# A planned clock for every engine, table lookups in VectorE's waits, and norms turned by VectorE and transfers

## The chip, the cores and the metric

One core of a Trainium2 chip. The metric is the device time of one execution in microseconds (us), the median of several runs. PE is TensorE, PEld its weight loads, DVE VectorE, ACT ScalarE, POOL GpSimd, SP the engine that issues most DMAs.

## The reference

Four layers, each wrapped the same way, over x of 2 x 512 tokens with 256 features, all in float32:

```python
x = x + layernorm(attention(layernorm(x), wq, bq, ...))   # 16 heads of 128, rope, causal softmax
x = x + layernorm(gelu_ffn(layernorm(x), packed 4-bit gate, up, down))   # 2048 hidden
x = x + layernorm(linear_attention(layernorm(x), W_qkv, W_out))
x = x + layernorm(silu_ffn(layernorm(x), lut[gate_idx], lut[up_idx], lut[down_idx]))  # 688 hidden
```

The linear attention takes `q = elu(q)+1`, `k = elu(k)+1` and running sums of `k` and of `k*v` along the tokens. It returns `q*sum(k*v)/(q*sum(k)+1e-9)`, projected by W_out. The last layer's three weight matrices are drawn from a table of 16 floats by 4-bit indices, so that each weight is a lookup.

## The kernel before

The tokens are cut into four units of 256 (`NUNIT`, `TU`); two units make one batch. An activation that TensorE multiplies has features on partitions and tokens along the free dimension: `xT1`, `xT2`, `xT3` for the gelu layer, the linear attention and the silu layer, each a tile of 128 partitions x 2 chunks x 256 tokens.

**The attention** is a loop of 34 slots (`slot`, L794), one head of one batch in each. A slot issues the score matmuls of head i, VectorE's masked minimum (L645), the exponentials (L663), the projections of q and k of head i+1 with rope (L584 to L620), the scaling by the inverse sums (L851), the output projection of head i-2, the values' sum of head i-1 (`attended`, L690), and last the turn of p: VectorE transposes in 32 x 32 blocks (L677), and four DMAs (L683) carry the blocks into `pT`. GpSimd adds the two halves of rope (L619, `qT` and `kT`), which the next slot's scores need. In the last slots, half blocks of the gelu layer's first unit fill TensorE.

**The later layers** run through generators. `ffn_hidden(u)` (L741) issues gate and up products of a unit in pairs of chunks, each pair with one gelu on ScalarE (L763) and one product on VectorE (L764). `ffn_out(u)` (L769) issues 64 matmul records of the down product and then begins a chain. `run` (L1038) steps through them, and after each step calls `poll` and issues one or two steps of the table lookups (`look_up`, L295). `silu_hidden` and `silu_out` do the same for the last layer.

**A chain** is a generator of small dependent work that is not on TensorE's main path. `after_ffn(u)` (L786) runs the norm (`norms`, L182) and then `linear_attention(u)` (L902), whose end is the norm of stage 3. `yield t` says that the next piece is due t us later. `poll` (L97) continues whatever is due by `now`, a clock that only TensorE's own matmuls move on (L118 to L124). The waits are fixed numbers such as 1.7, 2.4, 4.0, and 1.3 times as long while lookups remain (`slow`, L178). The order of all instructions on each engine is the order in which the program issues them.

**The norm between two layers** (L182 to L207) takes statistics of y for two halves of 128 tokens, adds the scaled y to x, takes statistics of the sum, normalises into `ln` on ScalarE (L197), and turns it: four TensorE transposes into PSUM (L200 to L203) and one ScalarE copy into `xT` (L204). Each unit has three such norms, twelve in all: stage 1 after the attention, 2 after the gelu layer, 3 after the linear attention. The small GpSimd steps of a norm are L167, L169 (a power) and L171.

**The lookups.** `wg` (2 pieces) is made during the attention by 16 compare-and-add steps each (L236 on VectorE, L240 on GpSimd), one or two per slot. `wu` (4 pieces of 320 columns) and `wd` (3 pieces of 512) are made by selection (`select_in`, L244): 19 VectorE instructions each, masks (L262, L279), eight pairs (L265) and seven picks (L275). They are issued after the attention, one or two after each TensorE step, whatever VectorE has to do. All must be done when the silu layer begins.

PSUM has four tags (`mm`, `s`, `t`, `o`) of two banks each. An output bank `o` of the last layer comes free when VectorE has added its scaled content to x (L176).

Of the kernel before, what the change touches and what calls it, by code (L numbers as in the profile page):

```python
# [34 lines left out]
NUNIT = B * NT // HT  # L35
INTER = 688
# [5 lines left out]
EARLY = 2  # L42
REST = INTER - (NO - 1) * P


@with_exitstack
def sandwich_kernel(
# [34 lines left out]

    def bank(tag):
        return psum.tile([P, 512], F32, tag=tag, name=f"ps_{tag}")
# [33 lines left out]
    def matmul(out, lhsT, rhs, start, stop, **more):  # L118
        nc.tensor.matmul(out, lhsT=lhsT, rhs=rhs, start=start, stop=stop, **more)  # L119
        now[0] += (math.prod(rhs.shape[1:]) / 0.6 + 5) / 1e3  # L120

    def transpose(out, in_):
        nc.tensor.transpose(out, in_, ident)  # L123
        now[0] += 0.11  # L124
# [3 lines left out]
    for t in range(NT):  # L128
        (nc.scalar if t % 2 else nc.sync).dma_start(
            out=x0[0][:, t, :], in_=x[0][t * P : (t + 1) * P, :]  # L130
        )
    cols_sb = const.tile([P, 3 * NH + 2 * NK], F32, name="cols_sb")
    nc.scalar.dma_start(out=cols_sb, in_=cols)
# [11 lines left out]
    nc.gpsimd.memset(mhalf, -0.5)  # L145

    nc.scalar.activation(small.tile([P, 1], F32, tag="ve", name="early"), mhalf[:, :1], AF.Identity)
# [10 lines left out]


    def stats(y, eps):  # L160
# [3 lines left out]
        nc.vector.bn_stats(st, y)  # L164
        nc.vector.bn_aggr(mv, st)
        ve = small.tile([P, 1], F32, tag="ve", name="ve")
        nc.gpsimd.tensor_scalar(ve, mv[:, 1:2], eps, None, ALU.add)  # L167
        rstd = small.tile([P, 1], F32, tag="rstd", name="rstd")
        nc.gpsimd.tensor_tensor(rstd, ve, mhalf[:, :1], ALU.pow)  # L169
        shift = small.tile([P, 1], F32, tag="shift", name="shift")  # L170
        nc.gpsimd.tensor_scalar(shift, mv[:, 0:1], rstd, -1.0, ALU.mult, ALU.mult)  # L171
        return rstd, shift

    def add_scaled(x, y, rstd):

        nc.vector.scalar_tensor_tensor(x, y, rstd, x, ALU.mult, ALU.add)  # L176

    def slow(t):  # L178

        return 1.3 * t if terms else t  # L180

    def norms(u, y, stage, to, eps=EPS, strided=False):  # L182
# [5 lines left out]
        yield 4.0 if terms and late else 1.7  # L188
# [4 lines left out]
        yield 5.0 if terms and late else 2.4  # L193
        n = acts.tile([P, HT, D], F32, tag="ln", name=f"ln{stage}_{u}")
        for j in range(HT):
            rstd, shift = second[j]
            nc.scalar.activation(n[:, j, :], x[j], AF.Identity, bias=shift, scale=rstd)  # L197
        yield 2.0 if terms and late else 1.3
        pt = bank("t")
        for kc in range(NK):  # L200
            for j in range(HT):
                part = n[:, j, kc::NK] if strided else n[:, j, kc * P : (kc + 1) * P]
                transpose(pt[:, kc * TU + j * P : kc * TU + (j + 1) * P], part)  # L203
        nc.scalar.copy(to.rearrange("p k t -> p (k t)"), pt)  # L204
        for j in range(HT):
            nc.scalar.activation(x[j], x[j], AF.Identity, bias=first[j][1])
        yield 0.6  # L207
# [11 lines left out]
    def look_up_in(scratch, pieces):  # L219
# [5 lines left out]
        def fetch(j):  # L225
            if j < len(pieces):
                nc.sync.dma_start(out=ix[j], in_=pieces[j][0])
# [3 lines left out]
        def term(j, i):  # L231
# [4 lines left out]
            nc.vector.tensor_scalar(  # L236
                e, ix[j], float(i), lut_sb[:, i : i + 1], ALU.is_equal, ALU.mult
            )
            if i:
                nc.gpsimd.tensor_add(to, to, e)  # L240
# [3 lines left out]
    def select_in(scratch, pieces):  # L244
# [4 lines left out]
        ix = [scratch[:, j % 2, : n[j]].bitcast(I32) for j in range(len(pieces))]  # L249
        words = lut_sb.bitcast(I32)  # L250

        def fetch(j):
            if j < len(pieces):
                nc.sync.dma_start(out=ix[j], in_=pieces[j][0])

        def piece(j):
            to = pieces[j][1].bitcast(I32)
            m0, m1, m2, *s = (scratch[:, 2 + i, : n[j]].bitcast(I32) for i in range(6))
            m3 = ix[j]

            def mask(m, bit):
                return lambda: nc.vector.tensor_scalar(m, ix[j], 1 << bit, None, ALU.bitwise_and)  # L262

            def pair(t, i):
                return lambda: nc.vector.tensor_scalar(  # L265
# [8 lines left out]
            def pick(t, m, other):  # L274
                return lambda: nc.vector.copy_predicated(t, m, other)  # L275

            def first():
                fetch(j + 1)
                nc.vector.tensor_scalar(  # L279
# [3 lines left out]
            return [  # L283
# [6 lines left out]

        fetch(0)
        for j in range(len(pieces)):
            terms.extend(piece(j))
# [8 lines left out]
    with ExitStack() as at:  # L302
# [9 lines left out]
        def load(name, gg):  # L312
# [6 lines left out]
            nc.sync.dma_start(out=wts[name, gg], in_=src[gg % NG])  # L319
# [3 lines left out]
        nc.sync.dma_start(out=cos_sb, in_=cos)  # L323
# [814 lines left out]
```

## Time and profile before

| | us |
|---|---|
| median of 3 runs (lowest, highest) | 647.89 (647.65, 648.43) |
| the profiled execution | 647.38 |
| its span, first to last instruction | 645.6 |
| its time outside the span | 1.8 |
| VectorE, ScalarE and GpSimd busy in it | 477.6, 302.2, 280.9 |

[...] A float32 matmul thus shows as two records (64 of `ps_o` for one unit's down product), while a transpose is one record. A record's duration is longer than the step from its start to the next record's start, because matmuls overlap: 128x256 records have a mean of 379 ns and follow each other at 216 ns. So what TensorE's work costs is read from the steps between starts, and a lost piece of time is a step that is longer than its kind's usual one.

### The profile page before, as it was taken

What the parts mean: (1) busy time and instruction counts of PE and PEld (TensorE: products, weight loads), DVE (VectorE), ACT (ScalarE), POOL (GpSimd) and SP (SyncE); (2) the same over time, 40 slices, a digit from 0 to 9 for tenths busy, and PEclk for the clock granted to TensorE, in tenths of its full rate; (3) what the DMA queues carried; (4) which work ended last, traced back from release to release, by engine and by line L of the source; (5) the groups of instructions that cost most, each with busy time, mean ns of one, the idle gap of its engine ahead of it and who ended that gap; (6) DMA issues with size and microseconds to landing.
All of it is one profiled execution on the core that took longest, in us unless ns stands there. A gap on an engine that the chain in (4) does not pass through costs nothing.

```text
span 645.6 us, 8157 instructions
## 1 busy us (share of the span) xinstructions
PE 628.7 (97%) x2542; PEld 467.9 (72%) x2542; DVE 477.6 (74%) x1107; ACT 302.2 (47%) x662; POOL 280.9 (44%) x342
## 2 busy tenths in 40 slices
PE   8899999999999999999999999999999999989896
PEld 6566666666666666666666788888888878868785
DVE  7869889877987988888787521874984995954743
ACT  3645666666555557566655721145026025225120
POOL 3344657454453565755675200441142152253531
PEclk9999999999999999999999999999999999989999
DMA  7456474555547455464534322000000000000000
GB/s 245 118 139 186 112 198 121 134 156 138 164 110 197 121 138 152 120 152 137 137 104 89 88 53 86 11 1 11 10 8 18 0 16 2 2 0 1 24 17 24
DMA packets 35754, 57.16 MB, mean 89 GB/s; under 512 B 4096, under 2 KB 23168, under 8 KB 35712
## 3 DMA queue, kind: packets, MB, share of 16 engines
q1 hardware_dynamic: 34992, 55.94, 32.5%
q10 hardware_dynamic: 720, 0.72, 0.5%
q8 instruction: 20, 0.33, 0.2%
q14 instruction: 22, 0.18, 0.1%
HBM read 28.33 MB, written 1.05 MB: 46 GB/s over the span
## 4 chain that ended last, share of the span: by engine, by line
PE 79%; DVE 12%; POOL 3%; ACT 3%; issue 2%; DMA 1%; ACTq 0%; POOLq 0%; DVEq 0%
PE ps_mm L119 32%; PE ps_s L119 17%; PE ps_o L119 15%; PE ps_t L119 12%; DVE scratch L265 1%; DVE den L957 1%; PE ps_t L123 1%; DMA pT<-turned 1%; DVE scratch L275 1%; POOL rstd L169 1%; PE ps_o L339 1%; DVE wd L275 1%; DVE rr L611 1%; DVE ra L608 1%; DVE st L164 1%
## 5 line engine op out<-in xcount | busy, mean ns | idle before, releaser
L240 POOL TENSOR_TENSOR wg<-wg,scratch 128x752 f32<-128x752 f32 x30 | 53.4, 1779 | 97.0 <-DVE scratch L236 97.0
L119 PE MATMUL ps_mm<-xT,wg 128*128 128x256 f32 (+1 forms) x352 | 85.1, 379 | 0.3 <-ACT q L926 0.3
L663 ACT ACTIVATE p<-p,mn 128x512 f32<-128x512 f32 (+3 forms) x128 | 70.6, 553 | 30.8 <-DVE mn L645 30.8
L119 PE MATMUL ps_s<-xT,wu 128*128 128x256 f32 x336 | 81.0, 379 | 0.0
L119 PE MATMUL ps_o<-wd,hT 128*128 128x256 f32 x352 | 77.9, 379 | 1.6 <-DVE x L176 1.6
L645 DVE CUSTOM_DVE_ANT_0 p<-ps_s,mask 128x512 f32<-128x512 f32 (+2 forms) x96 | 46.2, 510 | 40.1 <-PE ps_s L119 39.9
L119 PE MATMUL ps_t<-pT,v 128*128 128x512 f32 (+3 forms) x256 | 74.3, 433 | 1.5 <-DMA pT<-turned 1.5
L119 PEld LDWEIGHTS ps_o<-wd,hT 128*128 128x128 f32 x352 | 66.7, 190 | 11.0 <-DVE x L176 2.0
L119 PEld LDWEIGHTS ps_mm<-xT,wg 128*128 128x128 f32 (+1 forms) x352 | 66.3, 189 | 9.7 <-ACT q L926 0.7
L119 PEld LDWEIGHTS ps_s<-xT,wu 128*128 128x128 f32 x336 | 63.6, 190 | 8.5
L119 PEld LDWEIGHTS ps_t<-pT,v 128*128 128x128 f32 x256 | 48.6, 190 | 28.9 <-issue 15.3
L851 ACT ACTIVATE p<-p,rs 128x512 f32<-128x512 f32 (+3 forms) x128 | 61.4, 551 | 11.7 <-DVE rs L582 9.7
L119 PEld LDWEIGHTS ps_o<-wo,oT 128*128 128x128 f32 x256 | 48.6, 190 | 19.0 <-issue 13.6
L619 POOL TENSOR_TENSOR qT<-ra,rr 128x512 f32<-128x512 f32 x32 | 40.8, 1274 | 49.3 <-DVE rr L614 47.2
L119 PE MATMUL ps_s<-kT,qT 128*128 128x512 f32 (+2 forms) x192 | 60.8, 452 | 0.2 <-DVE kT L619 0.2
L119 PE MATMUL ps_o<-wo,oT 128*128 128x256 f32 x256 | 60.5, 379 | 0.0
L119 PE MATMUL ps_mm<-xT,wk 128*128 128x512 f32 x124 | 58.4, 593 | 0.6 <-ACT v L639 0.6
L119 PE MATMUL ps_mm<-xT,wq 128*128 128x512 f32 (+1 forms) x128 | 58.4, 580 | 0.2 <-ACT xT L420 0.2
L677 DVE STREAM_TRANSPOSE turned<-p 128x512 f32<-128x512 f32 (+3 forms) x128 | 54.1, 480 | 2.1 <-DMA pT<-turned 1.0
L119 PEld LDWEIGHTS ps_s<-kT,qT 128*128 128x128 f32 x192 | 35.9, 190 | 26.6 <-issue 16.0
L119 PE MATMUL ps_mm<-wv,xTv 128*128 128x256 f32 x232 | 54.9, 379 | 0.0
L764 DVE TENSOR_TENSOR hT<-ge,ps_s 128x512 f32<-128x512 f32 x32 | 21.9, 683 | 44.1 <-PE ps_s L119 33.9
(136 smaller groups left out, 1002.5 us busy)
## 6 DMA issues: line engine op xcount, KB each, us to landing
pT<-turned SPq DMA_DIRECT2D x126, 208.0 KB, 3.8
wo<-in_wo SPq DMA_DIRECT2D x17, 256.0 KB, 4.0
wq<-in_wq SPq DMA_DIRECT2D x16, 256.0 KB, 4.1
wk<-in_wk SPq DMA_DIRECT2D x16, 256.0 KB, 5.0
wv<-in_wv SPq DMA_DIRECT2D x16, 256.0 KB, 4.1
pk_g<-in_gate_p SPq DMA_DIRECT2D x4, 256.0 KB, 5.0
sc_g<-in_gate_s SPq DMA_DIRECT2D x4, 256.0 KB
pk_u<-in_up_p SPq DMA_DIRECT2D x4, 256.0 KB, 4.5
```

Of the source, the lines that this page charges most:

```text
L119: nc.tensor.matmul(out, lhsT=lhsT, rhs=rhs, start=start, stop=stop, **more)
L123: nc.tensor.transpose(out, in_, ident)
L164: nc.vector.bn_stats(st, y)
L169: nc.gpsimd.tensor_tensor(rstd, ve, mhalf[:, :1], ALU.pow)
L240: nc.gpsimd.tensor_add(to, to, e)
L275: return lambda: nc.vector.copy_predicated(t, m, other)
L619: (nc.gpsimd if i > 1 or kind == "q" else nc.vector).tensor_add(to, a, r)
L645: nc.vector.tensor_tensor_reduce(out=p[:, p_at[it] : p_at[it] + n], in0=ps, in1=mask[:, S - n :], scale=-scale, scalar=3e38, op0=ALU.add, ...
L663: nc.scalar.activation(pi, pi, AF.Exp, bias=mn[:, it : it + 1], scale=-1.0, accum_out=sums[i][:, it : it + 1],)
L677: nc.vector.transpose(turned[:, :, 3 * it : 3 * it + n, :].rearrange("p j t b -> p t j b"), p[:, p_at[it] : p_at[it] + n * P].rearrange("p ...
L764: nc.vector.tensor_mul(hT1[u][:, c2 : c2 + 2, :].rearrange("p c t -> p (c t)"), ge, pu)
L851: nc.scalar.mul(pi, pi, rs[i][:, it : it + 1])
```

## The change

An account of each engine's time takes the place of the single clock. `vector`, `scalar`, `pool` and `sync` wrap the four engines: every instruction issued through them is given a start (when its inputs are there and its engine is free[...]) and a cost from a table by kind and length; DMAs count 0.45 or 0.8 us to issue and 3.4 to land. Matmuls enter the same account. Chains no longer wait fixed times: `yield until(...)` waits until the account says that the named tiles are written.

The selection steps of `wu` and `wd` become `fills` of VectorE. Ahead of any VectorE instruction that would start late by the account, `fill` issues as many steps as fit before it, less 0.1 us. `wu` moves into the attention, from slot 17 on, in five pieces of 256 columns, with the first batch's `xT0` and `xTv` as scratch; `wd` stays after it. `flush` issues what is left: `wu` after the attention's slots, `wd` ahead of the silu layer. `wg` is made as before.

A norm is turned another way where `late` is filled (after the attention's slots) and it is not the last unit's stage 3. By the code these are nine of the twelve: two of stage 1, four of stage 2, three of stage 3 (the change's own words say ten). VectorE transposes 32 x 32 blocks into `tr`, and four DMAs on SP carry them into `xT`, as for p. The features then lie in another order on the partitions, so the host reorders the weights' rows, and the matmuls read `xT` through a strided view (`chunk`). The scales of the packed weights need two DMAs in place of one for gate and up. A norm that TensorE still turns has two smaller ScalarE copies.

Smaller edits: `values(1, 0)` is issued ahead of the first turn of p, the loads of the third q and k weights after the first `attended`; the reciprocal and product at the end of the linear attention go in four parts of 128 columns in place of two of 256; `silu_hidden`, `ffn_out` and `silu_out` yield more often, so that chains can come in between; up to four steps of the next `silu_hidden` in place of two are issued ahead of `silu_out`.

```diff
+    def start(self, who, outs, ins):
+        at = 0.0
+        for ap in (*outs, *ins):
+            name, lo, hi = self.part(ap)
+            at = max(at, self.floor.get(name, 0.0))
+            for a, b, end, write, by in self.seen.get(name, ()):
+                if by != who and a < hi and lo < b and (write or any(ap is o for o in outs)):
+                    at = max(at, end + 0.12)
+        return at
...
+class Engine:
+    def __init__(self, who, engine, times):
+        self.who, self.engine, self.times = who, engine, times
...
+    def cost(self, name, n, more, psum):
+        if self.who == "DVE":
+            if n <= 4:
+                return 0.15
+            return {
+                "tensor_scalar": 0.17 + n / (960 if psum else 1950),
...
+    def fill(self, until):
+        self.filling = True
+        while self.fills:
+            us, reads, write = self.fills[0]
+            if self.busy + us > until or (reads is not None and self.times.written(reads) > self.busy):
+                break
+            self.fills.popleft()
+            write()
+        self.filling = False
...
+            if name == "dma_start":
+                self.busy = max(self.busy, start) + (0.8 if len(outs) + len(ins) == 2 else 0.45)
+                self.times.add("DMA", self.busy + 3.4, outs, ins)
+                return write(*args, **more)
+            if self.fills and not self.filling:
+                self.fill(start - 0.1)
+            start = max(start, self.busy)
+            if self.other and not psum and name in Engine.HELD:
+                for a, b in self.other.spans:
+                    if a <= start < b:
+                        start = b
...
     def matmul(out, lhsT, rhs, start, stop, **more):
         nc.tensor.matmul(out, lhsT=lhsT, rhs=rhs, start=start, stop=stop, **more)
+        now[0] = max(now[0], times.start("PE", [out], [lhsT, rhs]))
         now[0] += (math.prod(rhs.shape[1:]) / 0.6 + 5) / 1e3
+        times.add("PE", now[0], [out], [lhsT, rhs])
     def transpose(out, in_):
         nc.tensor.transpose(out, in_, ident)
-        now[0] += 0.11
+        now[0] = max(now[0], times.start("PE", [out], [in_])) + 0.11
+        times.add("PE", now[0], [out], [in_])
+    def until(*aps):
+        return max(0.0, times.written(*aps) - now[0])
...
+    def chunk(t, kc):
+        return t[:, :, kc].rearrange("p a j t -> p j a t")
...
         x = [xs[u][:, j, :] for j in range(HT)]
         first = [stats(t, eps) for t in y]
-        yield 4.0 if terms and late else 1.7
+        yield until(*(t for f in first for t in f))
         second = []
         for j in range(HT):
             add_scaled(x[j], y[j], first[j][0])
             second.append(stats(x[j], EPS))
-        yield 5.0 if terms and late else 2.4
+        yield until(*(t for f in second for t in f))
         n = acts.tile([P, HT, D], F32, tag="ln", name=f"ln{stage}_{u}")
+        by_blocks = late and (u, stage) != (NUNIT - 1, 3)
         for j in range(HT):
             rstd, shift = second[j]
-            nc.scalar.activation(n[:, j, :], x[j], AF.Identity, bias=shift, scale=rstd)
-        yield 2.0 if terms and late else 1.3
-        pt = bank("t")
-        for kc in range(NK):
+            to_n, from_x = n[:, j, :], x[j]
+            if not by_blocks:
+                to_n = to_n.rearrange("p (k f c) -> p k f c", k=NK, c=4)
+                from_x = from_x.rearrange(
+                    "p (c f k) -> p k f c" if strided else "p (k c f) -> p k f c", k=NK, c=4
+                )
+            elif strided:
+                to_n = to_n.rearrange("p (k m) -> p k m", k=NK)
+                from_x = from_x.rearrange("p (m k) -> p k m", k=NK)
+            scalar.activation(to_n, from_x, AF.Identity, bias=shift, scale=rstd)
+        yield until(n)
+        if by_blocks:
+            tr = acts.tile([P, 4, NK, HT, 32], F32, tag="ln", name=f"tr{stage}_{u}")
             for j in range(HT):
-                part = n[:, j, kc::NK] if strided else n[:, j, kc * P : (kc + 1) * P]
-                transpose(pt[:, kc * TU + j * P : kc * TU + (j + 1) * P], part)
-        nc.scalar.copy(to.rearrange("p k t -> p (k t)"), pt)
+                vector.transpose(
+                    tr[:, :, :, j, :], n[:, j, :].rearrange("p (k c f) -> p c k f", k=NK, c=4)
+                )
+            for a in range(4):
+                sync.dma_start(
+                    out=to[:, a].rearrange("p k j t -> p (k j t)"),
+                    in_=tr[32 * a : 32 * a + 32].rearrange("f c k j t -> f c (k j t)"),
+                )
+        else:
+            pt = bank("t")
+            for kc in range(NK):
+                for j in range(HT):
+                    transpose(
+                        pt[:, kc * TU + j * P : kc * TU + (j + 1) * P],
+                        n[:, j, kc * P : (kc + 1) * P],
+                    )
+                scalar.copy(
+                    to[:, :, kc].rearrange("p a j t -> p j a t"),
+                    pt[:, kc * TU : (kc + 1) * TU].rearrange("p (j a t) -> p j a t", j=HT, a=4),
+                )
         for j in range(HT):
-            nc.scalar.activation(x[j], x[j], AF.Identity, bias=first[j][1])
-        yield 0.6
+            scalar.activation(x[j], x[j], AF.Identity, bias=first[j][1])
+        yield until(to)
...
+            picks = (4, 8, 9, 13, 16, 17, 18)
+            one, two = 0.19 + n[j] / 960, 0.17 + n[j] / 1950
+            return [
+                (one if i in picks else two, None if i else ix[j], step) for i, step in enumerate(steps)
+            ]
         fetch(0)
         for j in range(len(pieces)):
-            terms.extend(piece(j))
+            vector.fills.extend(piece(j))
...
+            if i == NH + 1:
+                flat = [
+                    [t.rearrange("p k c -> p (k c)") for t in (up_i, wu)],
+                    [t[0].rearrange("p k s -> p (k s)") for t in (xT0, xTv)],
+                ]
+                parts = [[t[:, at : at + TU] for at in range(0, t.shape[-1], TU)] for t in flat[1]]
+                select_in(
+                    parts[0] + parts[1],
+                    [tuple(t[:, at : at + TU] for t in flat[0]) for at in range(0, NK * FULL * P, TU)],
+                )
             now_in, done = i < NS, not (jobs or behind)
...
+            if i == 0:
+                values(1, 0)
+            elif i == 1:
+                load("q", 2)
+                load("k", 2)
...
+    vector.flush()
...
+        yield until(den)
         for ch in range(NK):
-            nc.vector.reciprocal(den[:, ch, :], den[:, ch, :])
-            nc.gpsimd.tensor_mul(lT[:, ch, :], v[:, ch, :], den[:, ch, :])
-            yield slow(1.9)
-        yield slow(2.0)
+            for t in range(HT):
+                part = ch, slice(t * P, (t + 1) * P)
+                vector.reciprocal(den[:, *part], den[:, *part])
+                pool.tensor_mul(lT[:, *part], v[:, *part], den[:, *part])
+                yield 0.3
+        yield until(lT)
...
```

## The prediction

> **What bounds the kernel now.** I read the page's engine shares and slices first, then the waits of TensorE, then the timeline of TensorE where those waits are, last the windows by stage.
>
> ```profile
> PE 628.7 (97%) x2542; PEld 467.9 (72%) x2542; DVE 477.6 (74%) x1107; ACT 302.2 (47%) x662; POOL 280.9 (44%) x342
> ...
> PEclk9999999999999999999999999999999999989999
> ```
>
> TensorE is busy 97% of the span, so only two things are to be had: work that leaves TensorE, and its few lost pieces. Adding up every matmul record at its kind's usual step (109 ns for 128 columns, 216 for 256, 429 for 512) gives 618.1 us. The remaining 27.5 of 645.6 are 1.4 before the first record, about 6 after the last one's start, and 20.0 of steps that are longer than usual. Of these 20.0, 8.6 lie before 35 us (warm-up, the first head); 11.4 lie behind 245 us. The waits show whom TensorE waited for:
>
> ```profile
> engine line waited for: us in total, times, longest us
> PE ps_t L123 <- ACT ln L197: 4.9, 4, 1.9
> PE ps_o L119 <- DVE x L176: 1.6, 1, 1.6
> ```
>
> The first row is the norms' transposes, placed in TensorE's order before ScalarE had their input. The timeline of TensorE shows the worst place, behind the last gelu unit:
>
> ```profile
> start us, us, engine line op out<-in xcount [idle before <-releaser]
> 569.04 1.03 PE L119 MATMUL ps_s<-xT,wu 128*128 128x256 f32 x4
> 572.00 0.33 PE L123 MATMUL ps_t<-ident,ln 128*128 128x128 f32 x1 [1.93 <-ACT ln L197]
> 573.32 0.90 PE L123 MATMUL ps_t<-ident,ln 128*128 128x128 f32 x3 [0.99 <-ACT ln L197]
> 574.01 3.16 PE L119 MATMUL ps_o<-wout_sb,lT 128*128 128x256 f32 x8
> 577.01 1.89 PE L119 MATMUL ps_mm<-xT,wqkv_sb 128*128 128x256 f32 x8
> ```
>
> Four records from 569.04 take 0.86, four transposes 0.45: TensorE loses 574.01 - 569.90 - 0.45 = 3.7. The eight records at 574.01 then take 3.00 in place of 1.73, as the clock granted in 572 to 577 is 0.66: another 1.3. Together 5.0.
>
> ```profile
> 606.51 0.59 PE L119 MATMUL ps_o<-wout_sb,lT 128*128 128x256 f32 x2
> 607.42 1.56 PE L119 MATMUL ps_o<-wout_sb,lT 128*128 128x256 f32 x6 [0.31 <-POOL lT L958]
> 610.63 2.86 PE L119 MATMUL ps_o<-wd,hT 128*128 128x256 f32 x12 [1.64 <-DVE x L176]
> ...
> 621.96 0.60 PE L123 MATMUL ps_t<-ident,ln 128*128 128x128 f32 x4
> ```
>
> Here are 0.5 for `lT` and 1.9 for an output bank that VectorE frees late. The rest of the 11.4: 1.4 at 529.6 and 1.6 at 248 to 273 (transposes that wait for `ln`), 0.6 at 583, and small ones.
>
> **Part 1: nine norms leave TensorE.**
>
> ```profile
> 430.91 1.06 PE L123 MATMUL ps_t<-ident,ln 128*128 128x128 f32 x8
> 431.81 1.89 PE L119 MATMUL ps_s<-xT,wu 128*128 128x256 f32 x8
> ```
>
> Eight transposes move the next matmul 0.90 us, so one costs 0.11. Nine norms by four: 36 x 0.11 = **-4.0**, on the bound engine, so all of it counts. Nine ScalarE copies (583 ns) go too, beside other work. Added are 18 VectorE transposes of 256 columns (403 ns in the rows of L677 by shape, so 7.3 us), which fit where VectorE idles (part 3), and 36 DMAs on SP. What those take is in the view of the tile `turned`, the same pattern with 208 KB:
>
> ```profile
> L683 SPq DMA_DIRECT2D pT<-turned x126: 543/642/1229, 24.6 to 380.5; - x126
> ...
> DMA to landing us min/median/max: 3.3/3.8/6.1
> ```
>
> Four issues of 0.64 one behind the other and 3.8 to land: the last lands some 5.7 behind the transposes, 6.5 behind `ln`, where transposes and copy took 0.45 + 0.58 plus TensorE's turn. [...] By the rows, only a norm on which TensorE waits pays for that; the others have 50 us of a unit's matmuls to hide in. One could pay: stage 2 of the last unit. I follow the rows, and test that one in part 2.
>
> Behind the new waits of SP stand index pieces of `wd` and output rows, which nobody needs soon. The strided view of `xT` costs nothing: `attended` reads `pT` with runs of 32 too, and its 512-column records step at 429 ns like the rest. The extra scale DMAs (8 at about 0.7 of SP) are issued ahead of p's turn, and SP then waits for VectorE anyhow; unhidden they would cost 0.7 in eight slots, below the 1.6 and more by which p lands early there.
>
> **Part 2: chains by account.** The last unit's chain sets whether TensorE can stay full behind the gelu layer. Before: `ffn_out(3)` ends at 563.2, first `wqkv` 577.0, the last at 587.2, `lT` and `wout` 606.5 to 609.0, transposes 622.0: 59 us. TensorE's own work in it is three silu units (11 products of 0.86 and 5.2 out: 14.7 each, 44), `wqkv` 5.2, two `wout` 3.5, transposes 1.3: 54 us. So it must idle, and the losses above are that.
>
> After, from the same rows. Stage 2: statistics, then six GpSimd steps per half (0.22, 0.57, 0.26 with gaps, 1.13 a set) to `ln` at 6.1; transposes, DMAs 6.5: about 13, against 13.8 now; the longer turn only eats what the waits in TensorE's order gave away. Linear attention: three projections with ScalarE between, 8.7; copy, table load 1.28, two exponentials 0.62: 11.8; GpSimd's sum 13.5; scans, products, scans 18.1; four reciprocals (3.5 in all) with GpSimd's quarter products 22.3; `wout` 24.5. Before it took 32, since 57 `wd` steps held VectorE up and fixed waits were too long. Stage 3 stays on TensorE: 8. Sum 46, and TensorE then has about 52 to do. It becomes the bound in this stage, with 6 to spare.
>
> So I take off: the 5.0 at 570 to 577 (**-5.0**), the 1.4 at 529.6, a norm that leaves TensorE (**-1.4**), 1.0 of the 1.6 at 248 to 273 (those norms stay on TensorE, but ask for the account's end of `ln` instead of 1.3 us) (**-1.0**), and 2.0 of the 3.1 at 583 to 611 (**-2.0**). The bank at 610.63 I leave half: silu's second output half needs the bank of the first whenever a `wout` takes the other, and an account sees that wait but does not remove it.
>
> What the exact waits may add: eight places (`wqkv` and `wout` of four units) where TensorE is now sent to data at the predicted end. Bounds: 0 (landing counted at 3.2 + 3.4 = 6.6 against 5.7 above) and 0.5 each, 4.0. I take **+0.8**, nearest the 0.5 of `lT` at 606.5 for one or two.
>
> **Part 3: lookups into VectorE's waits.** VectorE's room by stage:
>
> ```profile
> core 0: us, PE busy (x) PEld busy (x) DVE busy (x) ACT busy (x) POOL busy (x), PEclk, DMA share, GB/s
> 247.00:365.00 118.00, 117.11 (x426) 76.82 (x425) 93.54 (x226) 72.78 (x171) 71.45 (x61) 1.00 0.48 120
> 365.00:405.00 40.00, 40.00 (x180) 33.30 (x179) 11.10 (x26) 12.27 (x24) 0.81 (x3) 1.00 0.25 72
> 405.00:563.00 158.00, 156.82 (x740) 137.60 (x739) 123.06 (x255) 51.09 (x86) 50.20 (x96) 1.00 0.03 8
> ```
>
> `wu`'s rows add up to 35.0 busy (320 columns), so 95 shorter steps are about 37 for 24 + 29 us of room: enough, with some left to the flush. A flush of up to 10 us delays the last hidden product, which `ffn_out(0)` needs some 10 us later. Behind 405 VectorE loses 35 of its 123 and gains 7. On the path all this costs nothing while a step ends before VectorE's input comes. If the account is late, the next: GpSimd's `kT` (L619, 1.27) ends only 0.37 or 0.77 ahead of the first score matmul of alternate slots. Bounds: 0 and 0.5 in each of 15 slots, 7.5. A bound below nothing is excluded, as TensorE has no wait there. I take **+0.5**: the account's costs lie near the steps of the rows (pick of 320: 0.52 by formula, 513 ns).
>
> **Start.** `values(1,0)` ahead of p's first turn takes off ScalarE's 0.6 wait at 27, but TensorE waits at 31 for the same `pT`, whose ScalarE DMAs then issue 0.5 later. Bounds -1.7 (that wait gone) and +0.5; I take 0. The finer yields and quarter products are in part 2.
>
> **Sum.** -4.0 - 5.0 - 1.4 - 1.0 - 2.0 + 0.8 + 0.5 = -12.1. Span 645.6 - 12.1 = 633.5; outside it 1.8: 635.3 for a profiled execution. The median lay 0.5 above the profiled one: **635.8**.
>
> **Rivals.** *Everything works* (0.12): no new waits, the bank's 1.1 and the start's 1.7 gained too: 635.8 - 1.3 - 1.1 - 1.7 = 631.7, down to 631. *The last chain still binds* (0.14): if transfers and GpSimd's small steps make it 56 or more in place of 46, TensorE idles 4 or more of the 7 taken off there, and 2 elsewhere: 640 to 644. For it speaks that GpSimd's rows of a set are unchanged; against it that 10 us are then to be found. *The account does not meet the chip* (0.03): new waits of the size of the old, only part of the transposes' 4.0 gained, within 1 of 647.9. *Fills hold up rope* (0.07), the slower side: [...] (the longest L265 record is 1489 ns, the median 444), so that two such steps in a slot put `kT` 2 us late: less the slack, 1.4 by 15 slots = 21, against 12.1 gained: about 656. It decides from 0.8 us of TensorE wait per slot on.
>
> **Chances.** The forecast case (633 to 639) has 0.64. Faster by over 0.2%: 0.12 + 0.64 + 0.14 = 0.90; within 0.2%, about what a measurement of this kernel can tell from no change: 0.03; slower: 0.07. The range 631 to 641 takes the forecast, the better case and part of the third.
>
> **What would show it.** L123 with `ln` falls from 48 records to 12; no idle over 1 us in TensorE behind 405 except for one bank; `wqkv` of the last unit about 13 behind the end of its down product, `wout` about 24 behind that; L265 records between 237 and 405, none of `wu` behind 415. Fills are wrong if TensorE's waits list `kT` or `pT` behind 240; the chain is wrong if TensorE idles for `xT` or `lT` behind 560.

## The result and the profile after

| us | before | after |
|---|---|---|
| median (lowest, highest), 4 runs each on one chip | 647.77 (647.32, 648.43) | 637.94 (637.14, 639.89) |
| ratio to before, 95% interval | | 0.9852 [0.9828, 0.9876] |
| the profiled execution, and its span | 647.38, 645.6 | 638.02, 636.2 |

The change gains 9.8 us in the medians, where 12.1 were forecast. The span is 9.4 shorter. The page of the changed kernel:

```profile
PE 622.6 (98%) x2506; PEld 463.1 (73%) x2506; DVE 487.8 (77%) x1152; ACT 299.6 (47%) x656; POOL 275.1 (43%) x350
...
PEclk9999999999999999999999999999999999999999
```

TensorE has 36 records less (2542 to 2506): nine norms of four transposes. No slice of the span shows a granted clock below 0.9 any more (PEclk, in tenths; a digit is a fortieth of the span). In the changed kernel the wrappers give all instructions of an engine one line: L181 are VectorE, ScalarE and GpSimd, L163 the DMAs, L272 the matmuls, L278 the transposes. Its waits of TensorE, to be set beside the two rows of `ln` and `x` in the prediction:

```profile
engine line waited for: us in total, times, longest us
PE ps_t L278 <- ACT xT L181: 2.1, 3, 0.8
...
PE ps_o L272 <- DVE x L181: 1.5, 2, 1.1
...
PE ps_mm L272 <- ACT si L181: 0.7, 1, 0.7
...
PE ps_t L278 <- ACT ln L181: 0.2, 1, 0.2
PE ps_s L272 <- DVE kT L181: 0.2, 1, 0.2
```

The wait for `ln` fell from 4.9 to 0.2. A new one for `xT` stands in first place, and the bank (`ps_o`, freed by `x`) is about where it was. The timeline of TensorE shows both, with the last unit's chain:

```profile
257.85 0.38 PE L278 MATMUL ps_t<-ident,ln 128*128 128x128 f32 x2
259.06 0.44 PE L278 MATMUL ps_t<-ident,ln 128*128 128x128 f32 x2 [0.82 <-ACT xT L181]
...
573.11 3.62 PE L272 MATMUL ps_o<-wd,hT 128*128 128x256 f32 x16
576.57 1.89 PE L272 MATMUL ps_mm<-xT,wqkv_sb 128*128 128x256 f32 x8
...
590.41 1.13 PE L272 MATMUL ps_mm<-xT,wg 128*128 128x256 f32 x4 [0.73 <-ACT si L181]
...
603.91 1.99 PE L272 MATMUL ps_o<-wout_sb,lT 128*128 128x256 f32 x8 [1.15 <-DVE x L181]
...
611.44 2.86 PE L272 MATMUL ps_o<-wd,hT 128*128 128x256 f32 x12 [0.36 <-DVE x L181]
614.14 0.27 PE L278 MATMUL ps_t<-ident,ln 128*128 128x128 f32 x1
614.58 0.33 PE L278 MATMUL ps_t<-ident,ln 128*128 128x128 f32 x1 [0.17 <-ACT ln L181]
615.37 0.44 PE L278 MATMUL ps_t<-ident,ln 128*128 128x128 f32 x2 [0.46 <-ACT xT L181]
```

`wqkv` at 576.57 now follows the product before it without idling: the 5.0 at 570 to 577 is gone. The first pair of rows is new. In the norms that TensorE still turns, the changed loop copies chunk 0 into `xT` between the second and the third transpose, and the third waits for that copy: 0.99 beyond the usual step here, the same at 293, 0.68 at 615.

To see where the time went I took each step from one matmul record's start to the next, and counted what exceeds its kind's usual step, by stage. (The usual steps are taken 1 ns low, 215 for most 256-column records of 216. This puts some 2 us into each sum, 0.7 of it into the stage from 400 to 550, alike in all runs; differences stand.)

| lost pieces of TensorE, us | to 40 | 40 to 400 | 400 to 550 | from 550 | sum |
|---|---|---|---|---|---|
| before | 6.27 | 2.94 | 2.39 | 8.38 | 19.98 |
| after | 5.92 | 3.38 | 0.77 | 4.74 | 14.81 |

The 9.4 of the span are thus 3.9 of transposes gone (36 by 0.108), 5.2 of lost pieces and 0.3 behind the last record's start. That lookups left this stage shows in the window from 405 to 560, where VectorE was busy 123.06 of 158 before (405 to 563):

```profile
core 0: us, PE busy (x) PEld busy (x) DVE busy (x) ACT busy (x) POOL busy (x), PEclk, DMA share, GB/s
405.00:560.00 155.00, 155.00 (x720) 136.24 (x719) 100.51 (x203) 47.38 (x79) 47.70 (x104) 1.00 0.06 14
```

TensorE has no gap there at all.

### The profile page after: what moved, and what is told of

The parts are those of the page before. It is cut to its first block, busy times and chain, and to the rows that moved or that the text cites. A ratio compares the mean times of both kernels' runs of the same rounds, so it can differ in the third digit from the quotient of the medians.

```text
span 636.2 us, 8205 instructions
## 1 busy us (share of the span) xinstructions
PE 622.6 (98%) x2506; PEld 463.1 (73%) x2506; DVE 487.8 (77%) x1152; ACT 299.6 (47%) x656; POOL 275.1 (43%) x350
## 4 chain that ended last, share of the span: by engine, by line
PE 91%; DVE 4%; ACT 1%; DMA 1%; issue 1%; POOL 1%; ACTq 0%; POOLq 0%; DVEq 0%
PE ps_mm L272 37%; PE ps_s L272 20%; PE ps_o L272 20%; PE ps_t L272 13%; DMA pT<-turned 1%; PE ps_o L535 1%; DVE rr L181 1%; DVE den L181 1%; PE ps_t L278 0%; DVE x L181 0%; DVE st L181 0%; ACT L181 0%; DVE ra L181 0%; DVE ks L181 0%; POOL rstd L181 0%
## 5 line engine op out<-in xcount | busy, mean ns | idle before, releaser
L181 POOL TENSOR_TENSOR wg<-wg,scratch 128x752 f32<-128x752 f32 x30 | 53.5, 1784 | 98.7 <-DVE scratch L181 98.7
L181 DVE SCALAR_TENSOR_TENSOR rr<-ps_mm,cols_sb,sin_sb 64x512 f32<-64x512 f32 (+1 forms) x126 | 93.4, 741 | 2.6 <-ACT ra L181 0.2
L272 PE MATMUL ps_mm<-xT,wg 128*128 128x256 f32 (+1 forms) x352 | 85.4, 380 | 0.8 <-ACT si L181 0.7
L181 ACT ACTIVATE p<-p,mn 128x512 f32<-128x512 f32 (+3 forms) x128 | 70.6, 553 | 30.4 <-DVE mn L181 30.4
L272 PE MATMUL ps_s<-xT,wu 128*128 128x256 f32 x336 | 81.0, 379 | 0.0
L272 PE MATMUL ps_o<-wd,hT 128*128 128x256 f32 x352 | 78.2, 379 | 0.4 <-DVE x L181 0.4
L272 PE MATMUL ps_t<-pT,v 128*128 128x512 f32 (+3 forms) x256 | 74.3, 433 | 1.9 <-DMA pT<-turned 1.9
L272 PEld LDWEIGHTS ps_o<-wd,hT 128*128 128x128 f32 x352 | 66.8, 190 | 9.8 <-DVE x L181 0.8
L272 PEld LDWEIGHTS ps_mm<-xT,wg 128*128 128x128 f32 (+1 forms) x352 | 66.1, 189 | 10.7 <-ACT si L181 1.1
L181 DVE CUSTOM_DVE_ANT_0 p<-ps_s,mask 128x512 f32<-128x512 f32 (+2 forms) x96 | 46.0, 510 | 32.0 <-PE ps_s L272 31.6
L272 PEld LDWEIGHTS ps_s<-xT,wu 128*128 128x128 f32 x336 | 63.8, 190 | 8.7
L272 PEld LDWEIGHTS ps_t<-pT,v 128*128 128x128 f32 x256 | 48.6, 190 | 29.3 <-issue 15.3
L181 ACT ACTIVATE p<-p,rs 128x512 f32<-128x512 f32 (+3 forms) x128 | 61.4, 550 | 11.2 <-DVE rs L181 9.2
L272 PEld LDWEIGHTS ps_o<-wo,oT 128*128 128x128 f32 x256 | 48.6, 190 | 19.0 <-issue 13.6
L181 POOL TENSOR_TENSOR qT<-ra,rr 128x512 f32<-128x512 f32 x32 | 40.8, 1276 | 48.4 <-DVE rr L181 46.3
L272 PE MATMUL ps_s<-kT,qT 128*128 128x512 f32 (+2 forms) x192 | 60.8, 452 | 0.2 <-DVE kT L181 0.2
L272 PE MATMUL ps_o<-wo,oT 128*128 128x256 f32 x256 | 60.5, 379 | 0.0
L272 PE MATMUL ps_mm<-xT,wq 128*128 128x512 f32 (+1 forms) x128 | 58.4, 580 | 0.2 <-ACT xT L181 0.2
L272 PE MATMUL ps_mm<-xT,wk 128*128 128x512 f32 x124 | 58.3, 592 | 0.0
L181 DVE STREAM_TRANSPOSE turned<-p 128x512 f32<-128x512 f32 (+3 forms) x128 | 54.1, 481 | 2.1 <-DMA pT<-turned 1.0
L272 PEld LDWEIGHTS ps_s<-kT,qT 128*128 128x128 f32 x192 | 36.0, 190 | 26.8 <-issue 16.0
L272 PE MATMUL ps_mm<-wv,xTv 128*128 128x256 f32 x232 | 54.9, 379 | 0.0
```

The costliest lines, as they stand in the source:

```text
L181: return write(*args, **more)
```

## The experiments

My theory: the gain is TensorE's own work taken off, plus chains that end in time. The rivals are named at each group. All edits are to the changed kernel; ratios are to the kernel before, run on the same chip with the experiments of the same batch (its medians there 646.57 for e1 to e4, 647.03 for e5 to e8, 647.53 for e9 to e12). Between batches I compare ratios, 0.001 being 0.65 us.

| | median | ratio [95%] | lost: to 40 | 40-400 | 400-550 | from 550 |
|---|---|---|---|---|---|---|
| after | 637.94 | 0.9852 [0.9828, 0.9876] | 5.92 | 3.38 | 0.77 | 4.74 |
| e1 copies behind | 636.55 | 0.9842 [0.9820, 0.9864] | 7.81 | 1.32 | 0.78 | 4.50 |
| e2 wout in another bank | 637.35 | 0.9859 [0.9836, 0.9881] | 5.49 | 3.41 | 0.77 | 3.48 |
| e3 both | 634.17 | 0.9805 [0.9786, 0.9824] | 5.88 | 1.32 | 0.77 | 3.22 |
| e4 e1, all norms on TensorE | 653.27 | 1.0098 [1.0075, 1.0122] | 6.31 | 1.32 | 12.63 | 4.18 |
| e5 e4, slower account | 637.54 | 0.9857 [0.9840, 0.9874] | 5.99 | 1.35 | 0.97 | 2.11 |
| e6 e3, slower account | 641.25 | 0.9921 [0.9900, 0.9942] | 5.66 | 1.33 | 0.64 | 10.43 |
| e7 e3, last norm by transfers | 639.89 | 0.9897 [0.9877, 0.9917] | 5.57 | 1.33 | 0.78 | 8.94 |
| e8 fixed waits | 645.77 | 0.9980 [0.9967, 0.9992] | 7.74 | 6.91 | 2.94 | 5.72 |
| e9 e6, last unit on TensorE | 639.43 | 0.9875 [0.9860, 0.9890] | 7.57 | 1.34 | 0.64 | 6.42 |
| e10 e5, wout in another bank | 637.23 | 0.9854 [0.9836, 0.9872] | 5.52 | 1.31 | 0.96 | 2.09 |
| e11 wu behind the attention | 639.08 | 0.9880 [0.9865, 0.9895] | 6.26 | 3.40 | 0.64 | 5.60 |
| e12 fills late by 0.6 | 640.85 | 0.9897 [0.9881, 0.9913] | 5.74 | 5.40 | 0.64 | 4.73 |

**The two waits that are left (e1, e2, e3).** e1 makes one loop of transposes and one of copies behind it:

```diff
                         n[:, j, kc * P : (kc + 1) * P],
                     )
+            for kc in range(NK):
                 scalar.copy(
```

> The changed kernel, but a norm that TensorE still turns (three of twelve) issues its four transposes first and its two copies behind them. In the changed kernel's trace the third transpose waits for the first copy: 0.99 at 258, 0.99 at 293 and 0.68 at 614.6. Theory (TensorE is the bound everywhere, so each lost piece counts in full): these three pieces go, 2.5 us faster than the changed kernel, about 635.4. Rival (behind 560 the last unit's chain is the bound: 55 us from the end of its gelu layer to its last norm's transposes, against 51 of TensorE's work): the two pieces in the attention go, and the one at 614 comes back elsewhere or was on the chain itself, 1.5 to 2.0 faster. A third view: the pieces are no waits for the copy, but of the transposes themselves, and nothing changes.

The stage from 40 to 400 lost 1.32 in place of 3.38, so the copies are the cause of both 0.99. The third piece only moved: the product behind the transposes now waits 0.46 for `xT` at 615.5, as the rival had it. By the ratio e1 is 0.6 faster than the changed kernel, and the intervals overlap; in this profile the start lost 1.9 more (behind an idle stretch of 2.16 that ends at 32.6, fourteen records take 5.65, in the changed kernel 3.96), ahead of every norm that the edit touches.

e2 gives `wout`'s output another bank:

```diff
-        po = bank("o")
+        po = bank("t")
```

> The changed kernel, but the linear attention's output product uses a bank of the tag t, which is free behind the attention, in place of o. Theory: the waits for an output bank (1.31 at 602.4 ahead of wout, 0.52 at 610.7 in the silu output) go, and TensorE being the bound the run is 1.6 to 1.9 faster, about 636.2. Rival (the last unit's chain is the bound there): wout comes 1.3 earlier only if lT is there (GpSimd ends lT at 603.9, the bank came at 603.9 too), so at most 0.3 of the first and the 0.5 of the second are won: 0 to 0.8 faster.

Both bank waits (1.31 and 0.52) went from the trace, but a wait of 0.95 for `ln` at 611.9 came in their place: the silu product ran into the end of the chain. The profile gains 1.26 behind 550, the median is the same within its interval. e3 has both edits:

> Both edits: copies behind the transposes, and wout in a bank of tag t. Theory: the sum, 4.1 to 4.4 faster than the changed kernel, about 633.7, with no wait of TensorE over 0.5 behind 240. Rival (the chain binds behind 560): 2.0 to 2.8 faster, with a new TensorE wait for lT or ln behind 600.

It gives 634.17, by ratio 3.0 below the changed kernel, with intervals apart: the fastest version of the study. That lies between the theory's 4.1 to 4.4 and the rival's 2.0 to 2.8, with the rival's wait. Behind 240 it still waits for `si` (0.89), `ln` (0.95) and the last `xT` (0.63).

**What the transfers are worth (e4, e5).** e4 keeps all twelve norms on TensorE:

```diff
-        by_blocks = late and (u, stage) != (NUNIT - 1, 3)
+        by_blocks = False
```

> All twelve norms turned by TensorE again (copies behind the transposes, as in e1), chains by account and lookups in VectorE's waits as in the changed kernel: it undoes part 1 alone, and is to be compared with e1. Theory: 36 transposes of 0.11 come back on the bound engine, and the account places them where ln is there: 4.0 slower than e1 (3.5 to 5). Rival [...]: the norms get 5 us shorter, the last unit's chain falls from 55 to about 50, below TensorE's work, so the waits behind 560 (4.4) go: within 1 of e1. A second rival: TensorE again waits for ln at several norms, 6 or more slower than e1.

It is 16.7 slower than e1, not the 4 that the transposes cost, and slower than the kernel before. TensorE's wait for `ln` in it, and the timeline at the first gelu norm:

```profile
PE ps_t L278 <- ACT ln L181: 9.8, 9, 2.0
...
428.31 0.33 PE L278 MATMUL ps_t<-ident,ln 128*128 128x128 f32 x1 [1.86 <-ACT ln L181]
430.60 0.90 PE L278 MATMUL ps_t<-ident,ln 128*128 128x128 f32 x3 [1.96 <-ACT ln L181]
431.29 3.04 PE L272 MATMUL ps_s<-xT,wu 128*128 128x256 f32 x8
```

The account sends the transposes when it believes `ln` to be written, and it is 1 to 2 us early: it counts a small GpSimd step at 0.25 and a power at 0.57, where this trace has 0.28 and 0.33 in the mean, some 0.09 between two, and powers of 0.57 to 1.36 (0.66 in the mean); it counts ScalarE's strided normalising at 0.46, which takes 0.83. Eight records behind the waits take 2.88 in place of 1.73 (the mean granted clock of e4 is 0.996, of the changed kernel 0.999). So is it the place, or the route? e5 leaves the transposes on TensorE and corrects those costs:

```diff
-            return 0.57 if more.get("pow") else 0.25
+            return 0.8 if more.get("pow") else 0.38
```

with 0.37 more for a ScalarE step whose input is strided.

> As e4 (all twelve norms turned by TensorE, copies behind), with two costs of the account set to what the traces show: a one-column GpSimd step 0.38 in place of 0.25 and its power 0.80 in place of 0.57, and 0.37 more for a ScalarE activation that reads with a stride (834 ns against 602). e4 was 16.7 slower than e1, where 4.0 were expected: TensorE waited 9.8 for ln in 9 places. Theory: those waits come of an account that counts a norm's small GpSimd steps too short, so that transposes stand in TensorE's order 1 to 2 us early, while the route by transfers hides the same error, as it counts a landing 1.5 too long and puts nothing into TensorE's order at ln. Then the waits for ln fall below 3 and the run is 642 to 645, 5 to 8 above e1: the 4.0 of the transposes and some rest. Rival: the waits come of the norms' place on TensorE itself (ScalarE and GpSimd late from case to case, by 0.5 to 2), so a mean cost can't mend them: 649 or more.

It is 15.6 faster than e4 by the ratios, equal to the changed kernel (1.0 behind e1, its like with nine norms by transfers; the intervals overlap), and TensorE waits for `ln` once (an edit ahead has moved the lines by one):

```profile
PE ps_t L279 <- ACT ln L182: 0.2, 1, 0.2
```

So e4's waits were of its account, and with TensorE's norms well placed the transfers save little that the whole shows. What they do in the changed kernel is to take the step that needs an exact time out of TensorE's order: with four issues at 0.8 and 3.4 to land, the account counts 6.6, where 0.60 each and 2.2 to land (the view of the tile `tr`) make 4.0. The same account that is early for `ln` is 2.6 late for `xT`, and nobody waits.

**The last unit (e6, e7, e9, e10).** e6 puts e5's costs into e3:

> e3 (copies behind, wout in a bank of t) with the same two costs of the account as e5. Theory: e3's only waits of TensorE behind 240 are 0.95 for ln at 610, 0.63 for xT behind it and 0.89 for a silu at 587; of these the account can take the first by placing the transposes later, so 0.3 to 1.0 faster than e3's 634.2. Rival: later chains make the last unit's chain longer, and with the silu layer's work used up before it ends TensorE idles there: 0.5 to 2 slower than e3.

The rival had the direction, but 0.5 to 2: it is 7.5 slower than e3. All of it is behind 550 (10.43 against 3.22). The last unit's `wout` comes at 605.9, in e3 at 600.5; the silu products run out, and TensorE waits for `ln` 4.3 in two pieces; eight records behind them take 3.56 in place of 1.73 (the mean granted clock is 0.993, in e3 0.999). From `wqkv` to `wout` are 29.2, in e3 26.0. Most of these 3.2 is the place of `wout` in TensorE's order, which the account sets: it starts 1.0 behind the last piece of `lT`, in e3 1.3 ahead of it. e7 sends even the last stage 3 through transfers:

```diff
-        by_blocks = late and (u, stage) != (NUNIT - 1, 3)
+        by_blocks = bool(late)
```

> e3 with the last unit's stage 3 turned by VectorE and transfers too; TensorE's order is e3's without those four transposes. Theory [...]: in e3 the transposes stand at 611 and the silu product behind them at 612; by transfers xT lands 5 to 5.7 behind ln at 611.5, so TensorE idles about 4.5 to 5.5 there, less 0.4 of transposes and the 0.63 for the copy: 3.5 to 5 slower than e3. Rival (a turn by transfers is hidden everywhere, as in the other nine): 0.4 to 1 faster than e3.

It is 6.0 slower than e3. Its timeline of TensorE:

```profile
604.70 5.34 PE L272 MATMUL ps_o<-wd,hT 128*128 128x256 f32 x24
615.46 2.05 PE L272 MATMUL ps_mm<-xT,wg 128*128 128x256 f32 x4 [5.42 <-DMA xT<-tr]
617.30 1.91 PE L272 MATMUL ps_s<-xT,wu 128*128 128x256 f32 x4
```

TensorE idles for 5.4, then four records take 1.84 and the next four 1.70 in place of 0.86 (the mean granted clock is 0.994, in e3 0.999). From the end of VectorE's last transpose (611.2) to the product are 4.3, which the prediction put at 5.7 from rows of a larger tile; here nothing hides them. In e3, with the transposes on TensorE, the same place idles 0.95 for `ln` and 0.63 for `xT`: for this norm, where TensorE has nothing else to do, its own turn is the shorter one.

e9 sends all norms through transfers except the last unit's stages 2 and 3; e10 sends none. Both have e5's costs and `wout` in the other bank.

```diff
+        by_blocks = late and (u < NUNIT - 1 or stage == 1)
```

> e6 (copies behind, wout in a bank of t, the slower account) with the last unit's stage 2 on TensorE too, so that transfers turn eight norms, none of the last unit's chain. e6 was 7 slower than e3: TensorE idled 4.3 for ln of the last unit, as the slower account put that unit's chain later. Theory: with the last unit's two norms on TensorE its chain is some 1.5 to 5 shorter, and with the slower account the transposes stand where ln is there: TensorE waits under 2 behind 560, 632 to 635, as good as e3 or better. Rival: it is the slower account that delays the chain by itself, whatever turns the norm: 638 or more, with a wait for ln over 2 at the last norm.

> e5 (all twelve norms on TensorE, the slower account) with wout in a bank of t: the pair of e9 that differs in eight norms' turns alone. Theory of the prediction's part 1: 32 transposes of 0.11 are 3.5 on the bound engine, so 3 to 4 slower than e9. Rival (what was won by taking norms off TensorE is won as well by an account that is right, and the 3.5 go into other waits): within 1.5 of e9.

e9 was to be the best of both; it is no faster than e10 (2.2 slower by the medians, 1.4 by the ratios, with intervals that overlap), though e10 has 32 transposes (3.5 us) more on TensorE. The timelines of TensorE, first e9, then e10:

```profile
605.83 5.34 PE L273 MATMUL ps_o<-wd,hT 128*128 128x256 f32 x24
613.32 0.33 PE L279 MATMUL ps_t<-ident,ln 128*128 128x128 f32 x1 [2.15 <-ACT ln L182]
614.73 0.55 PE L279 MATMUL ps_t<-ident,ln 128*128 128x128 f32 x3 [1.08 <-ACT ln L182]
```

```profile
607.53 5.34 PE L273 MATMUL ps_o<-wd,hT 128*128 128x256 f32 x24
612.71 0.27 PE L279 MATMUL ps_t<-ident,ln 128*128 128x128 f32 x1
613.77 0.55 PE L279 MATMUL ps_t<-ident,ln 128*128 128x128 f32 x3 [0.79 <-ACT ln L182]
```

In both the last `ln` lets the second transpose go at about 614 (614.7 and 613.8). e10 spends more of the way there on work, e9 idles. At the end of the last gelu product e9 is still 3.0 ahead (557.9 against 560.9), about what 32 transposes take; at `wqkv` 1.7 (573.0 and 574.7); at `wout` it is 0.9 behind. So behind 550 the end is set by the last unit's chain, and here transposes taken off TensorE come back as idling. From `wqkv` to `wout` e9 takes 31.1, e10 28.5. VectorE's timelines, e9 and then e10, show a place:

```profile
587.71 0.69 DVE L182 TENSOR_TENSOR hT<-si,ps_s 128x512 f32<-128x512 f32 x1 [1.53 <-ACT si L182]
588.31 0.42 DVE L182 TENSOR_SCALAR ek<-ek 128x512 f32<-128x512 f32 x1
```

```profile
586.12 0.43 DVE L182 TENSOR_SCALAR ek<-ek 128x512 f32<-128x512 f32 x1 [0.18 <-ACT ek L182]
```

In e9 a silu product stands in VectorE's order ahead of `ek` and waits for ScalarE, which loads a table behind the exponentials first (1.28 in the changed kernel's trace); in e10 it stands behind. So `ek` is read 15.3 us behind `wqkv` in e9 and 11.4 in e10, of which 0.9 is a later third projection. e10 loses a part of that lead again, as its `wout` starts 1.8 behind `lT`. This is read from the traces; no run swaps the two instructions.

One pair speaks for the transfers. e3 (nine norms by transfers, the account as written) is 3.2 faster than e10 (none, the corrected account) by the ratios, with intervals apart; both have copies behind and `wout` in the other bank. The two edits don't add up: the corrected costs gain 15.6 with all norms on TensorE (e4 to e5), and lose 7.5 with nine by transfers (e3 to e6).

**The account itself (e8).** e8 puts fixed waits back into norms and linear attention, without the factor of 1.3 that the old ones had while lookups remained:

```diff
-        yield until(*(t for f in first for t in f))
+        yield 1.7
...
-        yield until(*(t for f in second for t in f))
+        yield 2.4
...
-        yield until(n)
+        yield 1.3
...
```

and in the linear attention 1.7, 4.0, 1.7, 1.7, 1.7, 0.95 (per quarter product) and 2.0; the wait for the transfers stays with the account.

> The changed kernel, but the chains wait the fixed times of before (1.7, 2.4, 1.3 in a norm; 1.7, 4.0, 1.7, 1.7, 0.95 and 2.0 in the linear attention; the landing of xT still by account); lookups stay in VectorE's waits and nine norms off TensorE. It takes the account out of the chains. Theory (most of the gain behind 405 is the norms leaving TensorE's order, and VectorE free of lookups; the exact waits add little): within 2 of the changed kernel's 637.9. Rival (the exact waits are what took TensorE's waits away, as the prediction put it): the waits for ln, lT and banks come back, 5 or more slower.

Only 0.2% is left of the gain: 8.3 slower than the changed kernel by the ratios, though the 36 transposes are off TensorE here too. The rival held. Its mean granted clock is 0.991, the changed kernel's 0.999: eight records behind a wait of 2.25 that ends at 32.5 take 3.91 (2.24 in the changed kernel), twelve behind one of 2.29 that ends at 618.7 take 4.38 in place of 2.59. Its waits of TensorE:

```profile
PE ps_o L272 <- DVE x L181: 2.3, 1, 2.3
...
PE ps_mm L272 <- ACT ge L181: 2.0, 1, 2.0
PE ps_t L278 <- ACT ln L181: 2.0, 3, 1.2
```

**The lookups (e11, e12).** e11 issues the five pieces of `wu` behind the attention, before `wd`:

> The changed kernel, but the five pieces of wu are not made in the attention: they stand before those of wd in VectorE's list, so all 152 steps fall into VectorE's waits behind the attention. Theory (VectorE idles 55 us in 405 to 560 of the changed kernel, and steps in its waits are free anywhere): within 1 of 637.9, with L265 records up to 560. Rival (moving wu into the attention freed VectorE for the chains): the flush ahead of the silu layer leaves 10 us or more at 560, just where the last unit's norm starts, and the run is 3 to 8 slower.

It is 1.1 slower in the median, 1.8 by the ratio, with intervals that overlap. VectorE is busy 134.5 of the 155 us from 405 on, and yet only one wait of TensorE grew: that for `si` at 590, by 0.87 to 1.6. Moving `wu` is worth 1 to 2, if anything. e12 lets every fill end up to 0.7 later than in the changed kernel:

```diff
-                self.fill(start - 0.1)
+                self.fill(start + 0.6)
```

> The changed kernel, but lookup steps may end up to 0.6 behind the start that the account gives VectorE's next instruction, in place of 0.1 ahead of it. It prices the rival of the prediction, lookups that hold VectorE up. Theory (TensorE has room of 0.2 to 0.6 at kT and of 2 or more at pT): VectorE's score and rope steps come up to 0.6 late in slots 17 to 31, TensorE waits for kT by 0 to 0.3 a slot, 0 to 5 slower than 637.9. Rival of the prediction: GpSimd's kT comes late by the whole 0.6 and more, 8 or more slower.

The waits of TensorE now have the row that the prediction named as the sign of fills in rope's way:

```profile
PE ps_s L272 <- POOL kT L181: 1.2, 2, 0.7
```

It is 2.9 slower by the ratio, with intervals apart: so VectorE's fills can hold rope up, as the slower rival said, but 0.7 late costs two slots, not fifteen. That rival reckoned with fills that put `kT` 2 us late; no run has those.

## Why the prediction was right, and where not

The sign and the range held (637.94 in 631 to 641). The mechanism held up to 550: the transposes are gone, and so are the waits for `ln`. Behind 550 it did not: TensorE was to be the bound there with 6 us to spare, and the last unit's chain still is. By its steps:

- *Nine norms, -4.0.* As work it is right: 36 records, 3.9. That "all of it counts" since TensorE is the bound failed: e5, with all twelve on TensorE, equals the changed kernel, and e10 is not slower than e9. Behind 550, work taken off turned into idling there; e3 against e10 shows that it need not all do so. And the step missed the larger role: with the account as written the same norms on TensorE cost 16.7 (e4 against e1).
- *The pieces at 570 to 577, -5.0, and at 529.6, -1.4.* Both came. From 400 to 550 the loss fell by 1.62.
- *The norms at 248 to 273, -1.0.* Failed: the stage from 40 to 400 lost 0.44 more. The `ln` waits went, but each copy stands between two transposes in the changed loop. The diff showed it, and I took the copies for "two smaller ScalarE copies". e1 proves it: 2.06 back.
- *583 to 611, -2.0.* Failed as a sum: the other losses behind 550 were 3.4 before and are 4.7 now. The bank stayed (1.83 at 602 and 611, 1.9 before), `si` waits 0.89 behind two table loads of 1.28 around the exponentials, and the turn at 614 to 616 loses 1.21.
- *Exact waits, +0.8.* The transfers' landings cost nothing, as they are counted too long (6.6, as the prediction says, for 4.0). What was dangerous was the opposite end, `ln`, which the prediction's bounds did not look at.
- *Lookups, +0.5.* They cost 0: `wu` is done at 402.1 as forecast, no wait for `kT` or `pT` behind 240, and `kT` has kept its lead of 0.37 and 0.77 in all but one slot (0.11).
- *Start, 0.* It gained 0.35: the 0.7 for the copy of v went, and the wait for `pT` grew from 1.69 to 2.07.
- *The last chain, 46 us.* Measured 55: 16.2 to `wqkv` (13), 29.2 on to the end of `wout` (24.5), 9.9 to the hidden products (8). The first 3.2 are mostly unit 2's stage-3 norm, whose small GpSimd steps stand among those of unit 3 from 560 to 570: the forecast priced the chain alone. In the second, the exponentials end 11.9 behind `wqkv`, as forecast (11.8), but `k`'s sum on GpSimd ends at 16.3 in place of 13.5: in VectorE's order a silu product waits in front of `ek` for ScalarE's table load, as in e9. Those 2.8 are the larger part of the 4.7. TensorE's own work in the 55 is about 51, so it idles where "6 to spare" was said; the rival that "the last chain still binds" had the mechanism, and 56 as its point, though the time fell among the forecast's.

By size: of 12.1 forecast, 9.4 came in the span; transposes 3.9 for 4.0, lost pieces 5.2 for a net 8.1, and 0.3 at the end that was not forecast. That the total is only 2.1 off is luck in part: the norms at 248 to 273 and the stage from 583 on missed by some 4.7 together, and the reserves of 0.8 and 0.5 that were not needed, with 0.35 each at the start and the end, made up for 2.

One sum of the prediction's opening does not come out. At the steps that it names (and 322 ns for 384 columns) TensorE's work is 620.3 us, not 618.1, and the lost pieces are 18.0, of which 6.2 and not 8.6 lie ahead of 35; 11.6 lie behind 245, and only these carry the forecast.

Open: whether a version with a shorter last chain (the silu product behind `ek`) would get the transposes' 4 us back, which wasn't tried; what the fills of `wd` are worth, as no run puts its steps back to where the old kernel issued them; and the smaller edits, the finer yields above all, which no run takes back.

## What to carry to other kernels

Before an instruction is placed in the order of the bound engine by an estimated time, ask what happens if the estimate is 1 us early: in e4 TensorE paid 9.8 of waits for that, while behind e1's transfers the same account cost it 0.2. Ask also whether the chain that ends the stage leaves room for work taken off the bound engine (e9 got nothing for 3.5 us of it), so price that chain with the neighbours that share its engines. And read a changed loop for the order in which it issues: one copy moved up between two transposes cost 2 us.

## What the runs showed of the hardware

- Behind some of TensorE's waits the records step slower, in runs whose mean granted clock is lower (e1 0.996, e7 0.994, e8 0.991, the changed kernel 0.999). It costs some 1.7 to 1.8 beyond the wait: fourteen records 5.65 for 3.96 at 32.6 in e1, eight 3.54 for 1.73 at 615.5 in e7, twelve 4.38 for 2.59 at 618.7 in e8. It does not come behind every such wait: eight records behind e4's wait at 32.7 take 2.23, as in the changed kernel. What decides it was not shown.
- In the kernel before, a VectorE step over a GpSimd instruction could last longer by it, which the account's `HELD` counts with: `eq` (L934, 128x512) took 1.54 in all four units, each time over GpSimd's 1.26 to 1.27 for `k`, and `ek`, of the same size with GpSimd idle, 0.43. The longest L265 record, 1.49, lies over GpSimd's 1.38 at 550.6; the median is 0.44.
- A GpSimd power took 0.57 in the median and up to 1.36 in e4 between 405 and 560, where VectorE's fills run. They cannot be the whole cause, which no run tried: in the kernel before, one of 0.91 stands at 599.9, 37 behind the start of the last selection step.
- ScalarE's normalising of 128x256 took 0.83 where it reads for a norm that TensorE turns (runs of 4x32x2), and 0.59 to 0.62 in the norms by transfers (the changed kernel).
- SBUF to SBUF transfers of 64 KB landed 2.2 us behind their issue (`tr` to `xT`), those of 208 KB 3.8 (`turned` to `pT`), medians of the changed kernel.
